# A residual added by accumulating transfers in place of GpSimd's additions, in the second layer of a two-layer convolution kernel

## The chip, the cores and the metric

The kernel runs on one core of a Trainium2 chip. A core has TensorE (PE, with PEld for its weight loads), VectorE (DVE), ScalarE (ACT), GpSimd (POOL), SyncE (SP) as an issuer of transfers, and 16 DMA engines. The metric is the device time of one execution in microseconds (us), the median of several runs; lower is better.

## The reference

Eight images `x` of 128 channels by 64 x 64 pixels, all in float32, go through two layers.

```python
# layer 0: deformable 3x3 convolution of the normalised image, batch norm, relu, residual
x = x + relu(batch_norm(deform_conv(group_norm(x))) * gamma + beta)
# layer 1: mixture of four 3x3 convolutions (two chosen per image) and a shared one, residual
x = x + moe_conv(group_norm(x))
```

In layer 1 each image's gate chooses two of four experts from the mean of its normalised channels. As a convolution is linear in its weights, the kernel mixes the weights for each image and does one convolution with them.

## The kernel before, in words

**First layer (`dense`, up to about 1371 us).** It computes the deformable convolution's output `y` for all eight images, writes it to DRAM (`ydram`, in the profile `yd`) and collects its batch statistics. Nothing of it is changed. (A second way through, `general`, is for large offsets and does not run on this input.)

**Second layer (`layer1`, from about 1372 us to the end at 1756).** For each image `b`:

1. *Load* (`load(b)`, L889 to L897): SyncE's queue brings `ydram[b]` into a tile `x1` and the image `x[b]` into a tile `xt`, each in four transfers of 512 KB. There are two tiles of each kind, taken in turn (`x1s`, `xts`). One of each pair lies in the buffers `pads` of the first layer, so the profile calls it `pad`, and the other `x` or `xt`.
2. *Prepare* (`prepare(b)`, L920 to L1063): for each of eight chunks `c` of 512 pixels, ScalarE applies the batch norm's affine and relu in place (L928), GpSimd adds the residual, `x1 += xt` (L930; for image 0 GpSimd and VectorE share the chunks), and VectorE takes the chunk's statistics two steps later (`bn_stats`, L932). Then come the statistics of the whole image (`mv`, L937), two tiny matmuls on TensorE which average them over the groups (`pm` L940, `pv` L950), the power on GpSimd (L111), the gate (`pg` L972 and some fifteen small VectorE instructions), the normalisation into a padded tile `pad2` on ScalarE (L963), the mixing of weights (`wmix`, L1039, and their Winograd-like sums `u`, L1050 to L1052), and the transformed rows `v` (L1018, L1020, L1022: sums and differences of even and odd rows) for four groups of rows.
3. *Products* (L1097 to L1126): four groups `g` of rows, in each four products `j` in the order 1, 2, 0, 3, in each three matmuls for the three columns of the filter: 16 products an image, into one of seven PSUM buffers `pc` each. `collect` (L1076) takes a product's result one product later: ScalarE copies product 1 with the bias into `t` (L1080), VectorE forms `s` and `d` from product 2 (L1084) and the two output rows from products 0 and 3 (`yo`, L1088 and L1090), and SyncE stores 512 KB to the output (L1092).

**What sets the order.** The layer is scheduled by hand: each engine executes in the order in which the Python code issues. `prepare(b + 1)` is a generator, and the loop over the products of image `b` moves it on by some `yield`s after each product (L1125: two after each of the first three products of a group, three after the fourth), so 36 steps an image. In the code before, the preparation of an image from 1 on has 33 steps: ten for the chunks (eight, and two for the delay of the statistics), ten for statistics, gate and the first half of the normalisation, four for the weights, one for `u`, eight for `v`. The matmul `pm` stands in TensorE's order right after product 5, `pv` after product 6 and `pg` after product 7; as TensorE is in order, the products behind them wait if their input is late. In the same way VectorE's `bn_stats` stand ahead of the combinations of later products.

For image 0 the preparation runs alone, ahead of the first product. `load(0)` is issued before the weights of the layer, `load(1)` after them, and `load(b + 2)` at the start of image `b`.

Of the kernel before, what the change touches and what calls it, by code (L numbers as in the profile page):

```python
# [8 lines left out]
F32 = mybir.dt.float32  # L9
I32 = mybir.dt.int32  # L10
AF = mybir.ActivationFunctionType
ALU = mybir.AluOpType
# [4 lines left out]
P = 128  # L17
H = W = 64
HW = H * W
# [3 lines left out]
CH = 512  # L23
NCH = HW // CH
# [33 lines left out]
def deform_moe_conv(  # L58
# [18 lines left out]
    nc = tc.nc  # L77
# [11 lines left out]
        out=gsel, in_=gsel, compare_op=ALU.is_ge, fill=0.0, base=0,  # L89
# [3 lines left out]
        out=gsel, in_=gsel, compare_op=ALU.is_ge, fill=0.0, base=3,  # L93
# [761 lines left out]
    def layer1():  # L855
# [6 lines left out]
        with ExitStack() as st:  # L862
            st.enter_context(tc.manual_schedule())
            b1 = st.enter_context(tc.tile_pool(name="b1", bufs=1))
# [8 lines left out]
                out=ident, in_=ident, compare_op=ALU.is_equal, fill=0.0, base=0,  # L873
# [6 lines left out]
                out=lower, in_=lower, compare_op=ALU.is_gt, fill=0.0, base=0,  # L880
# [3 lines left out]
            loaded = {}  # L884
            inside = [t[:, ROWPAD : ROWPAD + H].rearrange("p h w -> p (h w)") for t in pads]
            x1s = inside[0], b1.tile([P, HW], F32, name="x1")
            xts = inside[1], b1.tile([P, HW], F32, name="xt")

            def load(b):  # L889
                if b >= B:  # L890
                    return
                x1, xt = x1s[b % 2], xts[b % 2]
                for q in range(4):
                    part = slice(q * HW // 4, (q + 1) * HW // 4)
                    nc.sync.dma_start(out=x1[:, part], in_=ydram[b][:, part])
                    nc.sync.dma_start(out=xt[:, part], in_=x[b, :, part])
                loaded[b] = x1, xt  # L897

            load(0)
            sw_sb = b1.tile([P, TAPS, P], F32, name="sw_sb")  # L900
            ew_sb = b1.tile([P, NE, TAPS, P], F32, name="ew_sb")
# [11 lines left out]
            for e in range(NE):  # L913
                nc.sync.dma_start(out=ew_sb[:, e], in_=expert_w[:, e])
            load(1)

            experts = ew_sb.rearrange("p e (y x) o -> p e y x o", x=3)
            shared = sw_sb.rearrange("p (y x) o -> p y x o", x=3)

            def prepare(b, made):  # L920


                x1, xt = loaded.pop(b)
                stats = small.tile([P, NCH, 6], F32, name="stats")
                for c in range(NCH + 2):
                    if c < NCH:
                        y = x1[:, c * CH : (c + 1) * CH]
                        nc.scalar.activation(y, y, AF.Relu, bias=yshift, scale=yscale)  # L928
                        adder = nc.gpsimd if b or c % 2 == 0 else nc.vector
                        adder.tensor_tensor(y, y, xt[:, c * CH : (c + 1) * CH], ALU.add)  # L930
                    if c > 1:
                        nc.vector.bn_stats(  # L932
                            stats[:, c - 2, :], x1[:, (c - 2) * CH : (c - 1) * CH]
                        )
                    yield
                mv = small.tile([P, 2], F32, name="mv")
                nc.vector.bn_aggr(mv, stats)  # L937
# [98 lines left out]
                for kx in range(3) if b == 0 else (slice(0, 3),):  # L1036
                    part = wmix[:, :, kx]
# [28 lines left out]
            for _ in prepare(0, made):  # L1066
                pass
            for b in range(B):
                load(b + 2)
                ahead_of = prepare(b + 1, made) if b + 1 < B else iter(())  # L1070
                vs, us, bmix = made.pop(b)
                for g in range(NG):
                    yo = b2.tile([P, TR, 2, W], F32, name="yo")
                    part = {}
# [56 lines left out]

    dense()
    layer1()
    near_all = nc.values_load(count_i[0:1, 0:1], min_val=0, max_val=18 * 4 * B)
    with tc.If(near_all < 18 * 4 * B):
        general()
        layer1()
# [50 lines left out]
```

## Time and profile before

The median of three runs is 1756.35 us (1753.84 to 1756.67); the profiled execution spans 1756.5 us.

| what | number |
|---|---|
| TensorE busy | 1643.6 us, 94% of the span |
| VectorE busy | 1189.7 us, 68% |
| ScalarE busy | 944.4 us, 54% |
| GpSimd busy | 939.6 us, 53% |
| L930, GpSimd's additions into `x` | 32 in 47.0 us, 1496 ns each |
| L930, GpSimd's additions into `pad` | 28 in 39.6 us, 1442 ns each |
| L932, bn_stats | 672 ns each |
| bytes moved by DMA | 235.84 MB, mean 134 GB/s |

A share of busy time is an average over the two layers. In the forty slices of the span TensorE shows nines in the second layer but for two slices at the seam of the layers. The profile gives for each group of instructions its line, engine, output and inputs, count, busy time and mean length, and then how long the engine stood idle just ahead of it and who released it. A wait for several producers is put down to the one that came last. Windows of the span give the busy time of each engine in a stretch; a timeline gives start and length of instructions, merged where they follow one another.

### The profile page before, as it was taken

Reading aid. Unit: us, or ns where it says so; the run is one execution under the profiler, and the core shown is the slowest. Engines: PE = TensorE matmul, PEld = TensorE weight load, DVE = VectorE, ACT = ScalarE, POOL = GpSimd, SP = SyncE. Lnnn points to the kernel's source line nnn. Section 1 sums busy time; section 2 is a strip of 40 time slices with the busy share of each in tenths; the row PEclk is TensorE's granted clock in tenths of the full one; section 3 lists DMA queues with packets and bytes.
Section 4 is the critical chain, followed back from the end, with each engine's and each line's share of the span. In section 5 each row is a group of like instructions: output and inputs, shape, how many; then the busy total and the mean of one; then the engine's idle time right before and its main releaser. Section 6 shows DMA issues by size and latency. Waiting matters only on the chain. (4 is left out here: it accounts for less than half of the span.)

```text
span 1756.5 us, 21264 instructions
## 1 busy us (share of the span) xinstructions
PE 1643.6 (94%) x6490; PEld 931.0 (53%) x6490; DVE 1189.7 (68%) x1910; ACT 944.4 (54%) x1970; POOL 939.6 (53%) x1516
## 2 busy tenths in 40 slices
PE   4399999999999999999999999999999479999998
PEld 2155565566566556655665666566666234444443
DVE  4464874687467648755874587477665688888882
ACT  1465765576476557655765676476665323333330
POOL 3375576558557746764675657557763322322210
PEclk9599999999999999999999999999999689999999
DMA  4643774585368438744863675376663603444311
GB/s 133 124 121 93 154 179 106 115 194 137 93 133 203 121 82 168 180 106 103 193 150 94 134 187 143 98 137 151 161 158 87 267 25 144 155 156 154 123 49 62
DMA packets 197598, 235.84 MB, mean 134 GB/s; under 512 B 133964, under 2 KB 148048, under 8 KB 197478
## 3 DMA queue, kind: packets, MB, share of 16 engines
q0 software_dynamic: 94976, 124.94, 32.4%
q1 hardware_dynamic: 100556, 109.04, 20.7%
q8 instruction: 57, 0.93, 0.2%
q10 hardware_dynamic: 1946, 0.41, 0.1%
q14 instruction: 63, 0.52, 0.1%
HBM read 183.00 MB, written 50.82 MB: 133 GB/s over the span
## 5 line engine op out<-in xcount | busy, mean ns | idle before, releaser
L495 DVE TENSOR_TENSOR s<-xwts,ywts 100x324 f32<-100x324 f32 x968 | 691.5, 759 | 186.4 <-PE pq L506 160.1
L506 PE MATMUL pq<-s,xt 100*128 100x324 f32 x1936 | 696.8, 441 | 12.4 <-DVE s L495 6.7
L512 ACT COPY samples<-pq 128x324 f32<-128x324 f32 x968 | 423.9, 443 | 463.8 <-PE pq L506 458.1
L521 PE MATMUL py<-samples,dw_sb 128*128 128x384 f32 (+1 forms) x1584 | 625.1, 476 | 2.2 <-ACT y L532 2.1
L441 POOL DMA_DIRECT2D xwts<-tabx x863 | 527.2, 621 | 96.9 <-DMA ywts<-taby 52.6
L425 POOL DMA_DIRECT2D ywts<-taby x528 | 302.4, 587 | 365.8 <-DVE s L495 309.4
L506 PEld LDWEIGHTS pq<-s,xt 100*128 100x128 f32 x1936 | 322.4, 190 | 185.9 <-issue 48.7
L521 PEld LDWEIGHTS py<-samples,dw_sb 128*128 128x128 f32 x1584 | 299.5, 189 | 138.5 <-ACT y L532 6.5
L478 PE MATMUL pt<-ident,picked 128*100 128x128 f32 x968 | 194.2, 275 | 41.8 <-ACT picked L465 33.7
L478 PEld LDWEIGHTS pt<-ident,picked 128*100 128x100 f32 x968 | 121.6, 128 | 181.7 <-issue 80.0
L535 DVE BATCH_NORM_STATS2 ystats<-y 128x6 f32<-128x384 f32 (+1 forms) x88 | 48.2, 547 | 218.5 <-ACT y L532 218.5
L1102 PE MATMUL pc<-v,u 128*128 128x512 f32 x384 | 172.8, 599 | 9.2 <-DVE u L1051 9.2
L1102 PE MATMUL pc<-v,wmix 128*128 128x512 f32 x384 | 176.4, 605 | 0.0
L485 ACT COPY xt<-pt 100x512 f32<-100x512 f32 (+1 forms) x264 | 147.5, 559 | 2.2 <-PE pt L478 2.2
L313 PE MATMUL pc<-pad,offw_sb 128*32 128x504 f32 (+1 forms) x1152 | 142.2, 601 | 1.9 <-ACT pad L278 1.9
L1102 PEld LDWEIGHTS pc<-v,u 128*128 128x128 f32 x384 | 72.4, 190 | 98.3 <-issue 85.1
L1080 ACT ACTIVATE t<-pc,bmix 128x512 f32<-128x512 f32 x32 | 22.0, 687 | 182.5 <-issue 94.3
L1102 PEld LDWEIGHTS pc<-v,wmix 128*128 128x128 f32 x384 | 72.3, 191 | 88.6 <-issue 84.9
L457 ACT COPY picked<-pad 128x900 f32<-128x900 f32 x88 | 91.7, 1042 | 9.0 <-DMA xwts<-tabx 9.0
L608 ACT COPY samples<-samples 128x1188 f32<-128x1188 f32 x80 | 95.9, 1198 | 0.0
L930 POOL TENSOR_TENSOR x<-x,xt 128x512 f32<-128x512 f32 x32 | 47.0, 1496 | 85.3 <-ACT x L928 85.3
L930 POOL TENSOR_TENSOR pad<-pad,pad 128x512 f32<-128x512 f32 x28 | 39.6, 1442 | 71.6 <-ACT pad L928 71.5
(137 smaller groups left out, 897.1 us busy)
## 6 DMA issues: line engine op xcount, KB each, us to landing
ywts<-taby POOLq DMA_DIRECT2D x528, 116.0 KB, 4.3
pad<-in_x_dram SPq DMA_DIRECT2D x48, 512.0 KB
xwts<-tabx POOLq DMA_DIRECT2D x173, 116.0 KB, 3.8
out_dram<-yo SPq DMA_DIRECT2D x32, 512.0 KB
xwts<-tabx POOLq DMA_DIRECT2D x172, 92.8 KB, 3.8
yd<-y SPq DMA_DIRECT2D x80, 192.0 KB
xwts<-tabx POOLq DMA_DIRECT2D x173, 69.6 KB, 3.6
pad<-yd SPq DMA_DIRECT2D x16, 512.0 KB
```

Source lines behind the costliest of these rows:

```text
L313: nc.tensor.matmul(pc[32 * j : 32 * j + 32].rearrange("p (h w) -> p h w", w=W)[:, :, lo:hi], lhsT=offw_sb[:, k, :], rhs=pad[:, r : r + 8, ...
L425: engine.dma_start(out=y_wts[g % 2][r * Q : (r + NR) * Q, r].rearrange("p b c -> p (b c)"), in_=bass.AP(tensor=y_table[b].tensor, offset=y ...
L441: engine.dma_start(out=x_wts[g % 3][q:QQ:Q, :, lo:hi].rearrange("p t a b c -> p t (a b c)"), in_=bass.AP(tensor=x_table[b].tensor, offset= ...
L457: nc.scalar.copy(picked[g % 2][:, 1 : NT1 - 1], bass.AP(tensor=one.tensor, offset=one.offset, ap=[list(one.ap[0]), [T, NT1 - 2], [W, Q], [ ...
L478: nc.tensor.transpose(pt[0:QQ, c], picked[g % 2][:, c0 + c].rearrange("p y x -> p (y x)"), ident,)
L485: nc.scalar.copy(xts[g][0:QQ, c0 : c0 + n], pt[0:QQ, 0:n])
L495: nc.vector.tensor_tensor(s[0:QQ], x_wts[g % 3][0:QQ, c].rearrange("p a k r -> p k r a"), y_wts[g % 2][0:QQ, :, :, T * c : T * c + T].rear ...
L506: nc.tensor.matmul(pq.rearrange("p k r a -> p (k r a)"), lhsT=xts[g][0:QQ, c], rhs=ss.pop(n)[0:QQ].rearrange("p k r a -> p (k r a)"), star ...
L512: nc.scalar.copy(samples[g % 2][:, :, 2 : T + 2, T * c : T * c + T], pq)
L521: nc.tensor.matmul(py[:, first:], lhsT=dw_sb[:, 3 * ky + kx], rhs=samples[g % 2][:, n, first + ky : T + ky, kx : kx + W], start=(i == 0), ...
L608: nc.scalar.copy(samples[g % 2][:, :, 0:2], samples[(g - 1) % 2][:, :, T : T + 2])
L1102: nc.tensor.matmul(pc, lhsT=us[j][:, kx], rhs=vs[g][:, rows, kx : kx + W], start=(kx == 0), stop=(kx == 2),)
```

## The change

For images 1 to 7 the residual is no longer loaded into a tile and added by GpSimd. As soon as ScalarE has done relu on a pair of chunks, GpSimd's queue issues a transfer of 512 KB that reads `x[b]` from DRAM and adds it to `x1` as it writes (`accum_op=ALU.add`). So there are four such transfers an image. The statistics of a chunk are taken five steps after its relu instead of two, to leave time for the transfer; the preparation of these images so has 36 steps instead of 33, and `pm`, `pv` and `pg` move by three steps. Image 0 keeps the loaded `xt` and the additions shared by GpSimd and VectorE. One `xt` tile is left of the two, and SyncE's queue loads `x` for image 0 alone. The change is meant to take work off GpSimd, and with it a load into SBUF and the second `xt` tile.

```diff
-            xts = inside[1], b1.tile([P, HW], F32, name="xt")
+            xt = inside[1]
...
-                x1, xt = x1s[b % 2], xts[b % 2]
+                x1 = x1s[b % 2]
                 for q in range(4):
                     part = slice(q * HW // 4, (q + 1) * HW // 4)
                     nc.sync.dma_start(out=x1[:, part], in_=ydram[b][:, part])
-                    nc.sync.dma_start(out=xt[:, part], in_=x[b, :, part])
-                loaded[b] = x1, xt
+                    if b == 0:
+                        nc.sync.dma_start(out=xt[:, part], in_=x[b, :, part])
+                loaded[b] = x1
...
-                x1, xt = loaded.pop(b)
+                x1 = loaded.pop(b)
                 stats = small.tile([P, NCH, 6], F32, name="stats")
-                for c in range(NCH + 2):
+                late = 5 if b else 2
+                for c in range(NCH + late):
                     if c < NCH:
                         y = x1[:, c * CH : (c + 1) * CH]
                         nc.scalar.activation(y, y, AF.Relu, bias=yshift, scale=yscale)
-                        adder = nc.gpsimd if b or c % 2 == 0 else nc.vector
-                        adder.tensor_tensor(y, y, xt[:, c * CH : (c + 1) * CH], ALU.add)
-                    if c > 1:
-                        nc.vector.bn_stats(
-                            stats[:, c - 2, :], x1[:, (c - 2) * CH : (c - 1) * CH]
-                        )
+                        if b == 0:
+                            adder = nc.vector if c % 2 else nc.gpsimd
+                            adder.tensor_tensor(y, y, xt[:, c * CH : (c + 1) * CH], ALU.add)
+                        elif c % 2:
+                            part = slice((c - 1) * CH, (c + 1) * CH)
+                            nc.gpsimd.dma_start(
+                                out=x1[:, part], in_=x[b, :, part], accum_op=ALU.add
+                            )
+                    if c >= late:
+                        k = c - late
+                        nc.vector.bn_stats(stats[:, k, :], x1[:, k * CH : (k + 1) * CH])
                     yield
```

## The prediction

> **What bounds the kernel now.** I read the busy table and the chain first, then the second layer by stages, the waits in it, and the timelines of its start and of one steady image.
>
> ```profile
> PE 1643.6 (94%) x6490; PEld 931.0 (53%) x6490; DVE 1189.7 (68%) x1910; ACT 944.4 (54%) x1970; POOL 939.6 (53%) x1516
> PE 37%; DVE 2%; DMA 2%; ACT 1%; issue 0%; SPq 0%; DVEq 0%
> ```
>
> By stages (columns: window, its length, PE, PEld, DVE, ACT, POOL busy us, granted clock, DMA share, GB/s):
>
> ```profile
> 1380.00:1390.00 10.00, 1.73 (x6) 1.50 (x6) 6.80 (x24) 2.58 (x5) 2.83 (x4) 0.50 1.01 395
> 1400.00:1440.00 40.00, 28.78 (x64) 12.70 (x63) 33.01 (x63) 10.81 (x17) 11.48 (x7) 0.81 0.19 78
> 1480.00:1520.00 40.00, 40.00 (x98) 17.83 (x97) 34.66 (x57) 12.53 (x19) 11.64 (x9) 1.00 0.40 146
> ```
>
> From 1440 us on TensorE is busy all the time at full clock. Nothing taken from GpSimd can shorten that stretch; something added can lengthen it. What can be won lies in the start, 1392 to 1435. Its largest wait, and the timeline of TensorE there (start, length, engine, work):
>
> ```profile
> PE pm L940 <- DVE mv L937: 11.2, 1, 11.2
> ```
>
> ```profile
> 1397.61 3.75 PE L1102 MATMUL pc<-v,u 128*128 128x512 f32 x4 [9.24 <-DVE u L1051]
> ...
> 1409.85 5.31 PE L1102 MATMUL pc<-v,u 128*128 128x512 f32 x12
> 1426.38 0.59 PE L940 MATMUL pm<-mv,gsel 128*128 128x1 f32 x2 [11.22 <-DVE mv L937]
> 1426.84 5.38 PE L1102 MATMUL pc<-v,wmix 128*128 128x512 f32 x6
> 1432.06 0.28 PE L950 MATMUL pv<-e,gsel 128*128 128x1 f32 x2
> 1432.20 2.84 PE L1102 MATMUL pc<-v,wmix 128*128 128x512 f32 x6
> 1434.88 0.28 PE L972 MATMUL pg<-gw_sb,pooled 128*128 128x4 f32 x2
> ```
>
> I number the 16 products of an image (each three matmuls, six records, 2.6 us) from 0. TensorE has done products 0 to 5 of the first image and stands 11.2 us for `mv` of the second image, because the small matmul `pm` is next in its order. The following product takes 5.2 instead of 2.6 us: the clock is at half. Why VectorE is so late:
>
> ```profile
> 1394.52 2.84 POOL L930 TENSOR_TENSOR x<-x,xt 128x512 f32<-128x512 f32 x2 [2.71 <-ACT x L928]
> 1395.00 1.23 DVE L1050 TENSOR_TENSOR u<-wmix 128x128 f32<-128x128 f32 x1
> 1396.27 1.23 DVE L1051 TENSOR_TENSOR u<-u,wmix 128x128 f32<-128x128 f32 x1
> ...
> 1408.98 10.92 POOL L930 TENSOR_TENSOR x<-x,xt 128x512 f32<-128x512 f32 x6 [11.62 <-ACT x L928]
> ```
>
> ```profile
> L1018 DVE TENSOR_TENSOR v<-pad x31: 689/701/1767, 1406.1 to 1708.8; 128x528 f32<-128x528 f32 x31
> ```
>
> Beside GpSimd's additions the same VectorE work takes 1.77 instead of 0.70 us (minimum, median, maximum). In the steady state:
>
> ```profile
> 1501.22 4.33 ACT L928 ACTIVATE x<-x,yshift,yscale 128x512 f32<-128x512 f32 x6
> 1511.08 0.37 DVE L937 BATCH_NORM_AGGREGATE mv<-stats 128x2 f32<-128x48 f32 x1
> 1513.62 0.15 DVE L943 TENSOR_TENSOR d<-mv,pm 128x1 f32<-128x1 f32 x1 [2.17 <-PE pm L940]
> ```
>
> There `mv` is ready 1.8 us before TensorE reaches `pm` (1513.30), so nothing stands.
>
> **What the Trainium skill says.** "SBUF — State Buffer", section "Who interferes with whom": a VectorE instruction with two SBUF inputs contends with a GpSimd instruction that reads SBUF, the loser blocks. The trace agrees: 1.77 against 0.70 us. "TensorE: Matmul & The Clock Gate", section "What's actually happening": after an idle window of about 3.4 us the clock goes to half. Agrees: TensorE stops at 1415.2, the granted clock is 1.00 until about 1418.6 and 0.50 after. "Collectives: The Full Stack", section "The bandwidth ceiling: the fold count and why AG ≠ RS ≠ AR": a reducing transfer reads two sources for each write and so runs at half of a copy. This trace has no accumulating transfer. "DMA: Bandwidth & Descriptors", section "SWDGE vs HWDGE vs iDMA": accumulation goes through GpSimd's queue alone.
>
> **The change, part by part.**
>
> *GpSimd's additions for images 1 to 7 go* (56, 1.28 us each undisturbed), and with them the blocking of VectorE. At the start: L1050 and L1051 fall from 1.23 to about 0.29 us (the shortest in the trace), so the first product starts 1.9 us earlier, at 1395.7. Of the six `v` transforms of groups 2 and 3 five are blocked (1.78, 2.32, 1.77, 1.76, 2.31 against 0.70 and 1.25): 5.3 us. VectorE ends the transforms at 1418.7 − 1.9 − 5.3 = 1411.5. In the steady state the two blocked transforms of an image give 1.5 us of VectorE back, off the path.
>
> *bn_stats three steps later* (late 5). Three of the 36 steps that an image has now lie unused; after it 36 of 36 are used. `pm` moves from after product 5 to after product 6. VectorE must do in that order: two combinations of product 1, statistic 0, `yo`, statistics 1 to 3, `yo`, 4 to 7, two combinations of product 5, `mv`: 6 × 0.6 + 8 × 0.6 + 0.4 = 8.8 us. So `mv` is ready at 1411.5 + 8.8 = 1420.3 instead of 1426.35. TensorE ends product 6 at 1407.95 + 3 × 2.6 = 1415.8, stands 4.6 us, more than the 3.4 us, and I take the cold product (5.2 us): product 7 ends at 1420.3 + 0.55 + 5.2 = 1426.1. Before, it ended at 1434.88. **The start gains 8.7 us.** If the clock held, 2.6 more.
>
> *The later steps in a steady image* (times from the image's first matmul, T0 = 1497.81 in the old trace; product k ends at about 2.6(k+1)). The first mixing of weights comes after the combinations of product 9, at 29.5 us, where it was 24.6. From there the old order of VectorE runs 23.5 us up to the last `yo` of the image; less the combinations already done (1.2) and the lifted blocking (1.5) it ends at 50.3, that is 8.3 us into the next image; before it was 6.0. The operands of the next image's product 0 are ready at about 38.8 of 42.04: no wait. Then combinations, statistics, `yo` as above: `mv` at 8.3 + 9.1 = 17.4, including a wait for product 5. TensorE reaches `pm` at 15.5 + 2.6 = 18.1. Margin 0.7 us, where it was 1.8.
>
> *The accumulating transfers* (four of 512 KB an image, seven images). For the first pair of chunks relu runs some 6 us before T0, hidden. Pairs 2 to 4 have relus that end at 4.8, 6.3 and 7.7 us (the row at 1501.22, 0.72 us each). Issue costs GpSimd 0.6 us each, the nearest row (its DMA issues in layer one); GpSimd has nothing else queued but the `pow` far later. Queued behind a waiting bn_stats on VectorE are the PSUM combinations; with seven PSUM buffers TensorE does not feel these, but it feels `mv`. Rate: plain loads run at 395 to 420 GB/s, so half is 205 GB/s, 2.56 us a transfer; from the skill's 31 GB/s for each of 16 engines, halved, an estimate of 248 GB/s, 2.1 us. Fixed part 2.0 us (that DMA page, section "Anatomy of one DMA — SWDGE (gpsimd) path"; the quickest landing among GpSimd's DMAs here is also 2.0, the median 3.7 to 4.3 under load), split as one before and one after. A store of 512 KB falls among them, 1.3 us. The last lands at 4.85 + 1 + 3 × (2.1 to 2.56) + (0 to 1.3) + 1 = 13.2 to 15.8 us. After it come two statistics, two combinations and `mv`, 2.9 us: `mv` at 16.1 to 18.7, against 18.1. The stall at `pm` is 0 to 0.7 us an image; I take 0.3, six times (images 1 to 6 prepare another one, the first is counted above): +2 us. In the start the same sum puts the last landing at 1416 to 1417.4, and VectorE wants it at 1417.4: hidden.
>
> *Loads of x for images 1 to 7 leave the SyncE queue.* The same bytes move, later. At the start 4 MB less stand between 1378 and 1405; no compute waited for them. Zero, since VectorE's serial work covered it. Image 0 is unchanged.
>
> Sum: 1756.35 − 8.7 + 2 = **1750 us**.
>
> **Rivals.** (a) *The landing takes the place of the wait, no change*: with the fixed part at 3.3 us and the store in the way, the last lands at 17, the stall is 1.8, times six is 10.8: 1758. For it: medians above 3.6 us for GpSimd's transfers here; against: those have many small rows and a busy DMA. (b) *Slower*: the accumulation runs at a third of a copy, 137 GB/s, 3.8 us each. Last landing 4.85 + 2 + 11.5 + 1.3 = 19.7, stall 4.5, six times 27, the start gains some 5: 1756.35 − 5 + 27 = 1778. For it: no trace shows the rate, and statistics wait in order on an 87% busy VectorE. Against: the two-read account. (c) *More*: no stall, and TensorE stands so briefly that it stays warm: 1756.35 − 8.7 − 2.6 = 1745.
>
> **How the numbers follow.** Forecast (stall up to 0.75, 1747 to 1752.8) 0.50, (a) with stalls from 0.75 to 2 us 0.17, (b) above that 0.26, (c) 0.07. Faster by over 0.2% means under 1752.8: 0.57; same 0.17; slower 0.26. The range goes from (c) at 1745 well into (b), to a stall near 4: 1772; beyond it some 0.15.
>
> **What would show it.** Right: L930 on GpSimd for image 0 alone; L1050 at 1395 near 0.3 us; all long L1018 and L1020 gone; TensorE's wait for `mv` in the start near 5 us after seven products; a wait for `pm` of under 0.7 us in each later image. Wrong: bn_stats with idle time ended by the accumulating DMA, landings over 8 us after issue, TensorE under 100% at every image, or the matmuls of an image's product 0 waiting for `u`.

## The result, and the profile after

The changed kernel takes 1768.87 us (median of six runs, 1764.82 to 1771.65), the kernel before 1756.51 us beside it (six runs, 1750.45 to 1759.57): ratio 1.0073, 95% interval 1.0052 to 1.0094. It is slower by 12.4 us; the prediction said 6 us faster. The time lies in the predicted range, but at its slow end, which that range reached only by way of rival (b).

The busy table and the first line of the chain, after:

```profile
PE 1647.4 (93%) x6490; PEld 932.1 (53%) x6490; DVE 1173.6 (66%) x1910; ACT 943.3 (53%) x1970; POOL 879.3 (50%) x1488
PE 14%; DMA 4%; DVE 2%; ACT 1%; issue 1%; POOL 0%; DVEq 0%; ACTq 0%
```

GpSimd lost 60 us of work and VectorE 16, as meant; TensorE's work hardly changed, in a longer span, and DMA has 4% of the chain where it had 2%; by line these are the transfers of `x` that accumulate. The same two windows as before (length, PE, PEld, DVE, ACT, POOL busy us, clock, DMA share, GB/s):

```profile
1400.00:1440.00 40.00, 34.01 (x73) 14.79 (x72) 29.16 (x65) 11.92 (x18) 3.36 (x5) 0.87 0.40 90
...
1480.00:1520.00 40.00, 37.97 (x90) 16.56 (x89) 33.35 (x59) 12.23 (x18) 3.48 (x4) 1.00 0.56 145
```

Here the change reads at a glance. The start is better: TensorE works 34.0 of 40 us instead of 28.8. The steady stretch is worse: 2.0 us of a stretch that was full are idle, and that comes back with every image. The waits of the second layer (total us, times, longest):

```profile
PE pm L947 <- DVE mv L944: 33.0, 8, 14.2
...
DVE stats L941 <- DMA x<-in_x_dram: 11.3, 8, 1.8
DVE stats L941 <- DMA pad<-in_x_dram: 10.2, 6, 2.4
```

`bn_stats` now waits for the accumulating transfers (`x<-in_x_dram` and `pad<-in_x_dram`), 21.5 us in 14 waits, and TensorE stands for `mv` eight times (the longest, 14.2 us, is image 0's own, as before). The timeline of TensorE, at the start, and in two images:

```profile
1399.51 3.75 PE L1109 MATMUL pc<-v,u 128*128 128x512 f32 x4 [7.41 <-DVE u L1058]
...
1425.99 0.59 PE L947 MATMUL pm<-mv,gsel 128*128 128x1 f32 x2 [5.99 <-DVE mv L944]
1426.44 5.16 PE L1109 MATMUL pc<-v,wmix 128*128 128x512 f32 x6
...
1472.85 0.38 PE L947 MATMUL pm<-mv,gsel 128*128 128x1 f32 x2 [2.03 <-DVE mv L944]
...
1512.39 2.76 PE L1109 MATMUL pc<-v,wmix 128*128 128x512 f32 x6
1517.18 0.38 PE L947 MATMUL pm<-mv,gsel 128*128 128x1 f32 x2 [2.03 <-DVE mv L944]
```

VectorE and GpSimd ahead of that last line; the image's first matmul (T0) is at 1496.90:

```profile
1511.72 1.28 DVE L941 BATCH_NORM_STATS2 stats<-x 128x6 f32<-128x512 f32 x2 [1.83 <-DMA x<-in_x_dram]
...
1514.37 1.29 DVE L941 BATCH_NORM_STATS2 stats<-x 128x6 f32<-128x512 f32 x2 [1.36 <-DMA x<-in_x_dram]
1515.57 0.67 DVE L1091 SCALAR_TENSOR_TENSOR s<-pc,t 128x512 f32<-128x512 f32 x1
1516.16 0.68 DVE L1091 SCALAR_TENSOR_TENSOR d<-pc,t 128x512 f32<-128x512 f32 x1
1516.76 0.36 DVE L944 BATCH_NORM_AGGREGATE mv<-stats 128x2 f32<-128x48 f32 x1
```

```profile
1502.11 0.87 POOL L936 DMA_DIRECT2D x<-in_x_dram  x1 [9.43 <-DMA pad<-yd]
...
1504.93 0.86 POOL L936 DMA_DIRECT2D x<-in_x_dram  x1 [0.55 <-ACT x L930]
```

The chain is complete in these lines: last issue at 1504.93, its landing (1514.28) read at 1514.37 by two statistics, then two combinations and `mv`, then `pm` at 1517.18. TensorE had ended product 6 at 1515.15.

To see where the 12 us lie, I split each profile at the start of the first layer's last `bn_stats` (L535); what lies behind it I call "the layer".

| kernel | L535 ends the first layer at | span | layer | waits for `pm`: start; sum of images 1 to 6 |
|---|---|---|---|---|
| before | 1371.31 | 1756.5 | 385.2 | 11.2; 0 |
| after | 1375.07 | 1768.2 | 393.1 | 6.0; 12.9 |

The layer lost 7.9 us. Up to the first matmul of image 1 it won 7.0 (1455.78 before; 1452.57, or 1448.81 with the first layer's 3.76 taken off, after), and the images 1 to 6 lost 14.5, of which 12.9 are the six waits of 1.9 to 2.8 us; the tail adds 0.4. (A second profile of the kernel before, shown below, has a layer of 383.2; against it the loss is 9.9.) The other 3.8 us of the two spans are in the first layer, of which I speak at the end of the experiments.

### The profile page after: what moved, and what is told of

Same layout as the page of the kernel before. It is cut to its first block, busy times and chain, and to the rows that moved or that the text cites. A ratio compares the mean times of both kernels' runs of the same rounds, so it can differ in the third digit from the quotient of the medians.

```text
span 1768.2 us, 21236 instructions
## 1 busy us (share of the span) xinstructions
PE 1647.4 (93%) x6490; PEld 932.1 (53%) x6490; DVE 1173.6 (66%) x1910; ACT 943.3 (53%) x1970; POOL 879.3 (50%) x1488
## 5 line engine op out<-in xcount | busy, mean ns | idle before, releaser
L535 DVE BATCH_NORM_STATS2 ystats<-y 128x6 f32<-128x384 f32 (+1 forms) x88 | 48.2, 547 | 219.6 <-ACT y L532 219.6
L313 PEld LDWEIGHTS pc<-pad,offw_sb 128*32 128x32 f32 x1152 | 37.3, 109 | 73.5 <-issue 68.7
L936 POOL DMA_DIRECT2D x<-in_x_dram x16 | 14.1, 878 | 92.8 <-ACT x L930 72.8
```

Source lines behind the costliest of these rows:

```text
L313: nc.tensor.matmul(pc[32 * j : 32 * j + 32].rearrange("p (h w) -> p h w", w=W)[:, :, lo:hi], lhsT=offw_sb[:, k, :], rhs=pad[:, r : r + 8, ...
```

## The experiments

Theory: the last accumulating transfer lands too late for `mv`. Rivals: the three later steps alone do it, by VectorE's order; or the half rate has nothing to do with it, and it is the length of GpSimd's path or the stores beside it. The layers below are read as above.

**A plain copy in place of the accumulation** (`y` is overwritten by `x`: the residual's sum is left out).

```diff
-                                out=x1[:, part], in_=x[b, :, part], accum_op=ALU.add
+                                out=x1[:, part], in_=x[b, :, part]
```

> The changed kernel with its GpSimd transfers copying x over the activated y instead of adding it: the residual of images 1 to 7 in the second layer is computed wrongly in this run, y is lost. Measure: the second layer from the start of the last ystats statistics (L535) to the end, 385.2 us before and 393.1 changed. Theory L (the accumulating transfers land too late, because each takes 2.9 us of all DMA engines): a copy takes 1.3 us, the last lands some 5 us earlier, no statistics wait, TensorE stands under 0.3 us at pm in each of images 1 to 6, and the layer takes 376 to 379 us. Rival V (VectorE itself is late by the three later steps, the landing only coincides): TensorE still stands 1.5 us or more at pm of each image, layer 388 us or more. Rival F (the fixed part of a transfer from GpSimd's queue makes the landing late, not the adding): landings still 8 us, layer 390 or more.

Measured: 1753.81 us in a single run, layer 377.3, that is 15.8 less than with the accumulation, 13.0 of it in images 1 to 6. The wait for `pm` is 3.54 us at the start; later it is 0.34 and 0.13 us in two images, and none in the others. From issue to landing a transfer took, with the plain copy and in the changed kernel:

```profile
DMA to landing us min/median/max: 3.7/5.8/8.1
```

```profile
DMA to landing us min/median/max: 5.7/8.1/10.1
```

GpSimd's queue, the number and place of its issues and the later steps are all still there, and the loss is gone: what costs is that the transfer adds. It also speaks against VectorE's order alone, which is the same here and makes no wait. But the last copy landed at T0 + 15.3 (T0 1491.45), only 2.1 us before the accumulating one and not the 5 us expected. An issue was 0.33 us shorter, and these copies were slow for a time too: from 1499.80 to 1501.80 they moved 190 GB/s at a DMA share of 0.94, before a store moved beside them. So transfers from GpSimd's queue have slow stretches here whether they add or not; why is not shown.

**The later steps alone**, on the kernel before, with GpSimd's additions kept.

```diff
-                for c in range(NCH + 2):
+                late = 5 if b else 2
+                for c in range(NCH + late):
...
-                    if c > 1:
+                    if c >= late:
...
```

> The kernel before with only the statistics moved from two to five steps after the relu, GpSimd's additions kept. Layer measure 385.2 before, 393.1 changed. Theory L: the start gains some 1.4 us (pm stands one product later, but VectorE is still blocked by the additions). In later images GpSimd's additions now fall on more of the v transforms, which are three steps later, and each blocked one costs 1.07 us; three or four of them put mv some 2 us past pm, so about 395 us. If VectorE is blocked by only two as before, no stall and 384 us. Rival V: a stall of 2.4 us an image even without blocking, 398 us.

Measured: 1801.34 us (a single run), layer 424.4, 39 us more than before; the size was not foreseen. The wait in an image, and the product after it:

```profile
1479.97 0.59 PE L940 MATMUL pm<-mv,gsel 128*128 128x1 f32 x2 [4.25 <-DVE mv L937]
1480.41 4.89 PE L1102 MATMUL pc<-v,wmix 128*128 128x512 f32 x6
```

Six waits of 4.2 us are 25.4 us, and six products of 4.5 to 5.5 instead of 2.6 us, as the clock falls in each, some 14 more. Three steps later, the last `v` transforms of an image lie beside GpSimd's additions for the next one: four of them take 1.74 to 2.32 us. So the shift is only harmless together with the removal of the additions. This kernel can't speak for the shift without additions; the plain copy does.

**One step less and two steps more.**

```diff
-                late = 5 if b else 2
+                late = 4 if b else 2      # first kernel
+                late = 7 if b else 2      # second kernel
```

> The changed kernel with the statistics four steps after the relu. pm stays after product 6, but mv now stands ahead of the two combinations of product 5 in VectorE's order. Theory L: mv comes 1.2 us earlier after the same landing, the stall at pm falls from 2.1 to about 0.9 us in each of six images, and the layer takes 385 us (ratio to before 1.000). Rival V: one step less puts VectorE some 1.3 us ahead, which gives the same 1.2 us; but then statistics should not wait for a transfer, and under L they wait longer (some 2.5 us) than with five steps.

> The changed kernel with the statistics seven steps after the relu: 38 steps, so two run after the loop of products of an image; pm moves to after product 7, pv to after product 8. Theory L: TensorE reaches pm 2.6 us later, after the same landing; the stall of 2.1 us vanishes, the start stands some 3 us instead of 6 and may keep its clock; layer 375 to 379 us, time some 9 us below before (ratio 0.994 to 0.996). Rival V (the later the steps, the later VectorE): the tail of the preparation becomes late, TensorE stands at an image's first product waiting for u or v, the layer takes 393 us or more.

Measured: with 4, 1760.2 us, ratio to before 1.0014 (1.0004 to 1.0024), layer 385.1, waits of 0.8 to 1.2 us in the images, 5.9 in all. With 7, **1750.17 us, ratio 0.9952 (0.9933 to 0.9971)**, layer 372.9, and no wait for `pm` from image 1 on. TensorE with 7, at the start and in an image:

```profile
1425.45 0.38 PE L947 MATMUL pm<-mv,gsel 128*128 128x1 f32 x2 [2.71 <-DVE mv L944]
1425.69 2.82 PE L1109 MATMUL pc<-v,u 128*128 128x512 f32 x6
...
1509.62 0.28 PE L947 MATMUL pm<-mv,gsel 128*128 128x1 f32 x2
```

With 7, all of the gain lies in the start: up to image 1's first matmul the layer took 71.7 us, 12.7 less than before, while images 1 to 6 took 252.2 us in both kernels and the tail 0.5 more.

In an image the last pair of statistics starts at T0 + 17.27 with 4, T0 + 17.47 with 5 and T0 + 17.54 with 7 (T0 1492.37, 1496.90, 1488.94), and the landing itself is at T0 + 17.2, 17.4 and 17.5: it stays where it is. What moves is what stands around it. With 4, `mv` follows the pair at once (T0 + 18.6 instead of 19.9). With 7, a whole product more, 2.6 us, lies ahead of `pm` in TensorE's order.

**Six steps**, to see whether it is `pm`'s place that helps (`late = 6`).

> The changed kernel with six steps. pm goes behind product 7 as with seven, but pv too, so that TensorE does pm and pv with no product between and waits for VectorE's three small instructions (pm's end to pv's start was 0.5 us in the lone first preparation). Theory L: no landing stall, as with seven steps (372.9), but 0.5 to 0.8 us at pv in each image: layer 376 to 379. Rival V (each later step only costs): layer above 393.

Measured: 1754.61 us (a single run), layer 381.5, above the 376 to 379 expected. In an image:

```profile
1510.74 0.28 PE L947 MATMUL pm<-mv,gsel 128*128 128x1 f32 x2
1511.52 0.38 PE L957 MATMUL pv<-e,gsel 128*128 128x1 f32 x2 [0.50 <-DVE e L952]
```

`pm` stands behind product 7, as with 7 steps, and waits for nothing. But `pv` stands right behind it, with no product between, and TensorE waits 0.50 us for VectorE's two small instructions in each image. The start waits 3.71 us instead of 2.71, and the two products after it take 7.26 instead of some 5.5 us.

**The stores out of the way**, first by their place in the code: the stores of groups 0 and 3 are held and issued by SyncE with that of group 1 (`yo` in four buffers).

```diff
-                            nc.sync.dma_start(
-                                out=out[b, :, g * n : (g + 1) * n],
-                                in_=yo.rearrange("p t i w -> p (t i w)"),
-                            )
+                            held.append((out[b, :, g * n : (g + 1) * n], yo))
+                            if g in (1, 2) or b == B - 1:
+                                for dst, src in held:
+                                    nc.sync.dma_start(
+                                        out=dst, in_=src.rearrange("p t i w -> p (t i w)")
+                                    )
+                                held.clear()
```

> The changed kernel (five steps) with the stores of an image's group 3 and of the next image's group 0 held back to that of group 1, in four output buffers instead of two: the accumulating transfers of pairs 2 to 4 run without a store among them. Layer measure (last L535 to the end) 385.2 us before, 393.1 changed. Theory S (each of the three transfers takes 2.56 us of all DMA engines and the two stores among them 1.28 us each, which puts the last landing 17.4 us after the image's first matmul): without the stores the last lands at about 14.9, mv is ready at 17.8, under the 18.1 us of pm; no stall in images 1 to 6, one store less in the start as well; layer 377 to 379, time some 7 us below before. Rival A (the adding itself is slow, near 2.9 us a transfer, and stores pass beside it): landing near 16.7, stall some 1.4 us an image, layer 388 or more.

Measured: 1766.86 us, ratio 1.0062 (1.004 to 1.0084), layer 395.1, waits of 2.0 to 2.9 us. The edit did nothing: SyncE has nothing else in its order there, so it issued each store as soon as its data were ready, at the same moment as before (1505.28 beside 1505.15). So this run says nothing of the stores. In the next one ScalarE issues the held stores after it has made `t` of group 2, which fixes their moment:

```diff
+                            if g == 2:
+                                for dst, src in held:
+                                    nc.scalar.dma_start(out=dst, in_=src)
+                                held.clear()
...
-                            nc.sync.dma_start(
...
+                            if g in (1, 2) or b == B - 1:
+                                nc.sync.dma_start(out=dst, in_=src)
+                            else:
+                                held.append((dst, src))
```

> The changed kernel (five steps) with the stores of an image's group 3 and of the next image's group 0 issued from ScalarE's queue behind its activation for product 8, so that they start some 24 us after the image's first matmul, past the accumulating transfers. (Holding them back in the order of SyncE's queue alone had left them where they were, since that queue is idle and issues as soon as the data is there.) Layer measure 393.1 changed, 383.2 and 385.2 before. Theory S (three transfers of 2.56 us and two stores of 1.28 us share the DMA engines): the last landing moves from 17.4 to about 14.9, mv to 17.7, TensorE's stall at pm in images 1 to 6 from 2.0 to under 0.3 us; layer 378 to 380. Rival A (stores pass beside the transfers, which take 2.9 us each by themselves): landing 16.5 or later, stall 1.2 us or more, layer 387 or more.

Measured: 1760.2 us, ratio 1.0016 (1.0002 to 1.003), layer 384.3, waits of 0.6 to 0.9 us, 4.2 in all. Now three accumulating transfers are alone on the DMA engines, and windows of one us show them (columns as above), as does the read of their last landing:

```profile
1499.76:1500.76 1.00, 1.00 (x4) 0.48 (x3) 1.00 (x2) 1.00 (x2) 0.80 (x1) 1.00 0.76 102
1500.76:1501.76 1.00, 1.00 (x4) 0.46 (x3) 1.00 (x3) 0.32 (x1) 0.45 (x2) 1.00 0.93 139
1501.76:1502.76 1.00, 1.00 (x3) 0.38 (x2) 1.00 (x3) 0.00 (x0) 0.48 (x1) 1.00 1.00 197
...
1505.76:1506.76 1.00, 1.00 (x4) 0.45 (x3) 0.58 (x1) 0.25 (x1) 0.00 (x0) 1.00 1.07 209
1506.76:1507.76 1.00, 1.00 (x4) 0.50 (x3) 0.83 (x2) 0.44 (x1) 0.00 (x0) 1.00 1.09 217
```

```profile
1509.42 1.29 DVE L941 BATCH_NORM_STATS2 stats<-x 128x6 f32<-128x512 f32 x2 [1.20 <-DMA x<-in_x_dram]
```

At a DMA share of 1.0 they move 184 to 217 GB/s, where the loads of `ydram` just ahead move 406 to 426: half. The packets of the trace say the same: one of 4 KB took 328 ns when it accumulated and 159 ns in a plain copy (medians of 3584 packets each, changed kernel and plain copy). The first two us are slower, 102 and 139. The last pair of statistics starts at T0 + 16.07 (T0 1493.35), 1.4 us earlier than with the stores in between; six times that is 8.4 of the 8.8 us that the layer gained. Neither expectation was met: the first had the landing at 14.9 and the waits under 0.3 us, the second the landing at 16.5 or later and waits of 1.2 us or more. The stores cost 1.4 us, not 2.6; and alone the three transfers took 8.8 us, 2.9 each as the second had it, but by their slow beginning and not throughout.

**Relu and transfers of an image earlier**: two chunks a step instead of one, once with the statistics five steps later, once with four.

```diff
-                    if c < NCH:
-                        y = x1[:, c * CH : (c + 1) * CH]
+                    for i in (2 * c, 2 * c + 1) if b else (c,):
+                        if i >= NCH:
+                            continue
+                        y = x1[:, i * CH : (i + 1) * CH]
```

> The changed kernel (five steps) with two relus a step for images 1 to 7: chunks 0 to 3 and with them two transfers go out ahead of the activation of product 0, and two transfers instead of three fall into the stretch behind it. Layer measure 393.1 changed. Theory L: relus 4 to 7 end 6.3 us after the first matmul, the last transfer lands at 4.85 + 0.36 + 1.3 + 2 x 2.56 + one or two stores of 1.28 + 0.7 = 13.6 to 14.9; statistics do not wait beyond what VectorE is late anyway, no stall at pm; layer 377 to 379. Rival R (the landing is set by what is issued last, not by what queues ahead of it): the last is issued 1.4 us earlier, stall 0.6 us, layer 383.

> As the one before with four steps instead of five: mv stands ahead of the two combinations of product 5. Theory: as nothing waits for transfers, mv is 1.2 us earlier in the start than with five, TensorE stands some 3 us there instead of 4.5 and the clock may hold; no stall later; layer 373 to 376, ratio to before 0.994 to 0.996, like seven steps. Rival: VectorE waits for transfers again, being earlier in the order; layer 378 or more.

Measured: 1754.34 us, ratio 0.9989 (0.9977 to 1.0), layer 379.1, four waits in the images of 0.5 to 1.2 us; and 1750.34 us, **ratio 0.9962 (0.9947 to 0.9976)**, layer 376.9, two waits, of 0.5 and 1.1. Two of the four transfers are now issued about 5 us before T0, but they meet the four loads of the next `ydram` image (1484.95 on), and the last pair of statistics starts at T0 + 16.69, only 0.8 us earlier than in the changed kernel (five steps, T0 1490.19):

```profile
1506.88 1.28 DVE L943 BATCH_NORM_STATS2 stats<-x 128x6 f32<-128x512 f32 x2 [2.18 <-DMA x<-in_x_dram]
```

In other images it is earlier: the waits sum to 3.5 us with five steps, 9.4 less than in the changed kernel, and images 1 to 6 took 9.9 less. Up to image 1's first matmul the layer took 4.1 us less, as the wait for `pm` fell from 5.99 to 3.49 us and the product after it took 2.84 instead of 5.16, though TensorE came to `pm` some 0.9 us later. Together that is the gain in the layer, 14.0. With four steps the landing was not out of the way, as the expectation had it: VectorE's statistics waited 19.3 us for these transfers in all, and 10.3 with five.

**The change for image 1 alone**, to have the start's gain without the steady waits; with five and with seven steps for this image. The edit is against the changed kernel; the second `xt` tile is back.

```diff
-                    if b == 0:
+                    if b != 1:
                         nc.sync.dma_start(out=xt[:, part], in_=x[b, :, part])
...
-                late = 5 if b else 2
+                late = 5 if b == 1 else 2      # first kernel; 7 in the second
...
-                        if b == 0:
-                            adder = nc.vector if c % 2 else nc.gpsimd
+                        if b != 1:
+                            adder = nc.gpsimd if b or c % 2 == 0 else nc.vector
```

> The kernel before with the changed kernel's way (accumulating transfers, five steps) for image 1 alone; images 2 to 7 keep loads, GpSimd's additions and two steps. Theory: the whole gain of the change lies in the start, where image 1 is prepared, and the whole loss in images 2 to 7. So the start gains 7.0 us as in the changed kernel, no image stalls later, and the layer takes 378 us, the ratio to before being 0.996. Rival: part of the gain comes from the lifted blocking in later images; then it takes 380 us or more.

> As the one before with seven steps for image 1. Theory: in the start TensorE stands 2.7 us instead of 6.0 and keeps its clock, as in the changed kernel with seven steps, which took 372.9 us; nothing else of that kernel gained, so this one takes 373 us too, ratio 0.993 to 0.995. Rival: the additions of the later images cost something there that seven steps with transfers avoid; then 375 us or more.

Measured: 1764.16 us, ratio 1.0038 (1.0025 to 1.0051), layer 389.8; and 1762.52 us, ratio 1.0028 (1.0013 to 1.0042), layer 390.6. The wait at the start was 5.77 and 3.08 us (the product behind the 3.08 took 5.47 us, so the clock was not kept), and none came after image 2, but a new one stands at the seam between the two schedules. TensorE there with five steps:

```profile
1478.02 0.59 PE L947 MATMUL pm<-mv,gsel 128*128 128x1 f32 x2 [5.77 <-DVE mv L944]
1478.46 5.28 PE L1109 MATMUL pc<-v,wmix 128*128 128x512 f32 x6
```

The late `v` transforms of image 1 meet GpSimd's additions for image 2 (1.73 and 2.31 us), and `pm` of image 2 is back behind product 5. With seven steps the wait is 9.40. Neither was foreseen: a change for one image shifts what lies under the next.

**The kernel before once more, unchanged.**

> The kernel before, unchanged, to see how far the first layer alone differs from one profile to the next: its last statistics (L535) start at 1371.3 in the first profile and at 1372.7 to 1375.2 in five others whose first layer has the same order of instructions. Theory: this is chance, and it falls anywhere from 1371 to 1376; the second layer takes 385.2 again, within 0.3. Rival: the changed kernels lengthen the first layer; then it stays at 1371 to 1372.

Measured: 1754.09 us (a single run), layer 383.2, 2.0 less than in its first profile, where 0.3 was expected: four instead of five `v` transforms at the start were blocked, and the wait for `pm` was 9.97 instead of 11.22. The first layer ended at 1369.24, earlier than either expectation.

**What stays open.** The first layer holds the same instructions in the same order in before and after, and its last L535 starts at 1369 and 1371 in the two profiles of before, at 1375 in that of after, and from 1370 to 1378 in the others. Both ends of that range, 1370.40 and 1378.31, come from the two kernels with the change in image 1 alone, which have the same first layer and the same tiles; so differences of this size need no cause in the kernel. The layer explains 7.9 of the 12.4 us; that the rest is chance is likely from this, but not shown.

## Why the prediction was wrong

The failed step is the last landing: "The last lands at 4.85 + 1 + 3 × (2.1 to 2.56) + (0 to 1.3) + 1 = 13.2 to 15.8 us." It was at T0 + 17.4. The rate in the middle of that sum was right; the terms around it were mis-sized (most of all the way to the first byte, 0.9 us too short), and a slow beginning of 1.1 us had no term. Term by term, from the image at T0 1496.90:

- *Half rate*: right, at the slow end. The Trainium skill, "Collectives: The Full Stack", "The bandwidth ceiling: the fold count and why AG ≠ RS ≠ AR", gives half for a reducing transfer, and 184 to 217 GB/s against 406 to 426 agree: 3 × 2.56 = 7.7 us.
- *From the relu to the first byte*: 4.85 + 1 was 5.85. The issue began some 0.3 us after the relu and took 0.87 (not 0.6), and the first bytes moved at 1503.68, T0 + 6.8: 0.9 more than I took.
- *The first bytes*: the transfers began slowly, with 90 and 98 GB/s in the two windows of one us from 1503.30. Where they were alone (stores issued by ScalarE) they took 8.8 us from first to last byte instead of 7.7, so 1.1 were lost. I had no such term.
- *Stores*: I allowed for none to one. One falls in whole (group 3 of the previous image, issued at 1505.15) and a part of the next (group 0, issued some 5 us later): up to the last accumulated byte, at 1513.90, they had moved 0.70 MB. Taking both away was worth the 1.4 us measured above, just over the largest value allowed.
- *From the last byte to the landing*: 0.4 us (1513.90 to 1514.28), where I took 1. The fixed part of 2.0 us by the Trainium skill, "DMA: Bandwidth & Descriptors", "Anatomy of one DMA — SWDGE (gpsimd) path", fits as a whole: 1.6 us from the issue to the first byte and 0.4 behind the last. But I had split it evenly, and the page puts most of it behind the last byte; here most of it lies ahead.

6.8 + 1.1 + 7.7 + 1.4 + 0.4 = 17.4; it closes of itself, as the 1.4 is the difference between the two kernels' landings. Behind the landing came 2.9 us up to `pm` (2.9 forecast), and TensorE reached `pm` at T0 + 18.25 (18.1): a wait of 2.0 us instead of 0.3, six of them 12.9 us instead of 2. So the mechanism named was right, and the terms for the landing were mis-sized. It is rival (a)'s wait (1.8 us, 10.8 in all). That the time is still 10 us above that rival's 1758 comes in the main from the start (1.7 us less won), the images (14.5 instead of 10.8 lost) and the first layer's 3.8.

The other steps:

- *Additions gone at the start*: right. L1057 took 0.29 us, the long transforms are gone, and with the first layer's 3.76 us taken off, the first product started at 1395.75 (1395.7 forecast) and the transforms ended at 1411.4 (1411.5).
- *The start's last landing, "hidden"*: wrong, by the same terms. It came at 1419.3, with 3.76 taken off (1416 to 1417.4 forecast), `bn_stats` waited 0.66 and 1.20 us there, and `mv` came at 1422.2, again with 3.76 taken off (1420.3). So the start gave 7.0 instead of 8.7 us. That the product after it would be cold was right (5.16 us).
- *VectorE's order in an image*: right. The last `yo` ends at T0 + 8.2 (8.3), no product waits for `u`, and `mv` less the 3.2 us of waiting would be at T0 + 16.7 (17.4).
- *Rival (c)*: with seven steps its mechanism is what happened. The start stands so briefly that the next product takes 2.82 us, no image waits, and the layer gains 12.3 us (11.3 by the rival's sum), though in another kernel than the one forecast.

Rival (b)'s third of a rate, 137 GB/s, is excluded by the 184 to 217; that the time came out on its side of the kernel before was luck for that rival, since a wait of 2 us an image is enough. The chance of slower, 0.26, rested on that rate alone: I had costed the landing from its nearest ends and left the queue of small terms, nearly all in the same direction, out of the middle value.

## What to carry to other kernels

A transfer that replaces an addition moves work from an engine with room to a landing that somebody waits for: write down the time of the last landing term by term, with every other transfer in that window, and compare it with the moment at which the in-order engine needs it. When the landing can't be moved, move the reader: two steps more turned a loss of 0.7% into a gain of 0.5%, with the landing where it was. (The gain is the start's alone: where TensorE is busy throughout, nothing was won.) And look at the neighbours of a shifted instruction on its own engine, as `pv` behind `pm` and the transforms beside the additions show.

## What was unexpected of the hardware

- An accumulating transfer costs GpSimd 0.86 us to issue; as a plain copy, 0.53.
- An accumulating packet of 4 KB took 328 ns on its DMA engine, a plain one 159 ns (medians).
- The accumulation starts slowly, at 66 to 140 GB/s in its first two us in three profiles, though the DMA engines show a share of 0.7 to 1.0 there. The plain copies from the same queue had a slow stretch as well (190 GB/s at a share of 0.94), so the adding need not be its cause.
- After a wait of TensorE the clock did not fall by its length alone. The product behind it took 2.8 us after waits of 2.71 and 3.49, but 4.2, 5.5 and 4.5 after 2.84, 3.08 and 3.54, and 5.2 after 5.99. The Trainium skill, "TensorE: Matmul & The Clock Gate", "What's actually happening", has a window of 3.4 us that runs freely, so that a gap just above it may or may not hold a whole one. That fits the 3.49, and the granted clock stayed at 0.50 for 3.4 us after the waits of 2.84 and 3.54 and for 6.8 after those of 3.08 and 5.99, one and two such windows. Why the clock fell after 2.84 and 3.08 at all is not shown. The changed kernel's steady waits of 1.9 to 2.8 us left it at 1.00.
